# Attention on TensorE: scores and weighted sums over all four channel quarters in turn, in bursts of half a group

## The chip, the core and the metric

The kernel runs on one core of a Trainium2 chip. The metric is device time in microseconds (us): the median of five runs is 6176.71 us (6159.52 to 6181.42). One further execution was recorded by the hardware profiler. Engines are named as in the profile: PE is TensorE (matmuls), PEld its weight loads, DVE is VectorE, ACT is ScalarE, POOL is GpSimd, and SP issues most transfers.

## What is computed

A network of four residual layers on an image tensor of 8 x 56 x 56 x 192 in fp32. Two layers mix tokens by Toeplitz products, the third is a depthwise convolution with an MLP, the fourth is a windowed attention. Only the fourth is touched. Its reference, cut to what matters (x is the group-normalized input):

```python
WS, DISP, N_HEAD, DIM_V, DIM_MODEL = 7, 3, 6, 32, 192
x = jnp.roll(x, (-DISP, -DISP), (1, 2))
b, n_h, n_w, _ = x.shape
wh, ww = n_h // WS, n_w // WS
q, k, v = x @ Wq, x @ Wk, x @ Wv
shp = (b, N_HEAD, wh * ww, WS * WS, DIM_V)          # a plain reshape
q, k, v = q.reshape(shp), k.reshape(shp), v.reshape(shp)
scores = jnp.einsum('bhnqd,bhnkd->bhnqk', q, k) * DIM_V ** 0.5
scores = scores + bias
scores = scores.at[:, :, -ww:].add(LOWER_MASK)
scores = scores.at[:, :, ww - 1:ww].add(RIGHT_MASK)
attn = jax.nn.softmax(scores, axis=-1)
out = jnp.einsum('bhnqk,bhnkd->bhnqd', attn, v)
out = out.reshape(b, n_h, n_w, -1) @ Wfc + bfc
out = jnp.roll(out, (DISP, DISP), (1, 2))
```

So there are 8 x 6 x 64 small attentions of 49 queries by 49 keys, each over 32 channels.

## The kernel before

**Units and groups.** The attention (function `attention`, from L1061) works through 16 units: eight images by two halves of the tokens. A unit is cut into NG = 3 groups of 64 small attentions. The 32 channels of an attention lie on one quarter of the 128 partitions: quarter 0 to 3 hold different attentions, and a group has 16 of them on each quarter.

**One group, by function.**
- `scores` (L1253) is called twice, for i = 0 and i = 1. A call does quarters i and i + 2: for each of 8 windows, two halves (64 rows of the output) and the two quarters it multiplies 32 x 64 weights from `qf` with 32 x 49 columns from `kf` into one PSUM tile `s`. Then comes the softmax's first part: DVE scales and adds the bias (L1274) and takes the maximum (L1283), POOL subtracts it (L1284), ACT takes the exponential (L1285).
- `divide` (L1288): DVE sums (L1292) and takes the reciprocal (L1293), POOL multiplies (L1294).
- `turned` (L1296) transposes the probabilities of the group before on PE (L1300); the copy to SBUF, `et`, is made by DVE for i = 0 (L1310) and by ACT for i = 1 (L1308).
- `weighted` (L1313), also called for i = 0 and i = 1, multiplies 49 x 32 weights from `v` with 49 columns from `et` into the PSUM tile `po`, and `sixths` (L1330) copies `po` out by DVE (L1332) and rearranges it by ACT (L1337).

Scores thus use tiles of the array of 32 rows by 64 columns, and a call touches four of the eight such tiles. Weighted sums use tiles of 64 rows by 32 columns, again four of eight in a call.

**Pieces between.** `project` (L1170) is a generator that makes the next unit's `v`, `qf` and `kf` in ten pieces: four for `v` (L1179, L1189; copied out by ACT, L1197, and sent through DRAM), six for `qf` and `kf` (L1232; copied out by DVE, L1247, and ACT, L1245). `out` (L1341) is the output projection of the unit before, in two pieces (L1348; added to the input by DVE, L1359). The loop (L1402 on) puts such pieces between the bursts, by the table `order` at L1401: in group 0 four pieces of `v`; in group 1 a piece of `qf`, then the first piece of `out` with a piece of `qf`, then the second piece of `out`; in group 2 the last four pieces. The order in a group is

```
scores 0, piece 0, divide 0, scores 1, piece 1, divide 1,
transposes 0 and 1, piece 2, weighted 0, piece 3, weighted 1
```

where transposes and weighted sums belong to the group before (`late`). The loop runs once more after the last unit, for the weighted sums and the output that are left. At the end of group 2 the unit after next is normalized (L1154 on DVE, L1162 on ACT).

**PSUM.** Every PSUM tile comes from `bank2`, four tiles of two banks used in rotation, so a tile can be written once the fourth before it has been read. The instructions of an engine are issued in the order that the framework's scheduling gives; on PE this is the source's order here, on DVE mostly so.

Of the kernel before, what the change touches and what calls it, by code (L numbers as in the profile page):

```python
# [33 lines left out]
def view(ap, offset, dims):  # L34

    return bass.AP(ap.tensor, ap.offset + offset, [ap.ap[0], *dims])


class Net:
# [1021 lines left out]
    def attention(self, L, xs, gn3, gnd, ys, vd):  # L1061
# [6 lines left out]
        nc, tc, inp = self.nc, self.tc, self.inp  # L1068
# [4 lines left out]
        WR = 49  # L1073
        NG = 3
        p = self.at1
        if True:
            one = lambda name, shape: p.tile(shape, F32, name=name, bufs=1)
            bank2 = self.bank2
            gr = [one(f"gr{i}", [128, 4, 2]) for i in range(2)]

            def load_gr(i):
                for half in HALF:
                    nc.sync.dma_start(gr[i][half], gnd[i].rearrange("(b c) s -> c b s", c=C)[128:C])
# [166 lines left out]
                    fs.append(f)  # L1250
                return v, fs[0], fs[1]

            def scores(hh, g, i, qf, kf):  # L1253


                s = bank2()
                for n in range(8):
                    for half in range(2):
                        for c in range(2):
                            qd = slice(32 * (i + 2 * c), 32 * (i + 2 * c) + 32)  # L1260
                            u = (16 * g + 8 * half + n) * WR
                            nc.tensor.matmul(
                                s[64 * half : 64 * half + 64, c, n * WR : (n + 1) * WR],
                                qf[qd, u : u + 64],
                                kf[qd, u : u + WR],
                                start=True,
                                stop=True,
                            )
                var = {0: 1, 3: 2}.get((2 * i + 3 * hh + g) % 4, 0)
                e = ering[count[0] % NE]  # L1270
                count[0] += 1
                ev = e[:, :, :, :WR]
                e3 = e.rearrange("p c n k -> p (c n) k")[:, :, :WR]
                nc.vector.scalar_tensor_tensor(  # L1274
                    ev,
                    view(s, 0, [[512, 2], [WR, 8], [1, WR]]),
                    math.sqrt(32.0),
                    view(bias, var * 8 * WR, [[0, 2], [WR, 8], [1, WR]]),
                    ALU.mult,
                    ALU.add,  # L1280
                )
                mx = p.tile([128, 16], F32, name="mx", bufs=6)
                nc.vector.tensor_reduce(mx, e3, AX.X, ALU.max)  # L1283
                nc.gpsimd.tensor_sub(e3, e3, view(mx, 0, [[1, 16], [0, WR]]))  # L1284
                nc.scalar.activation(e3, e3, AF.Exp)  # L1285
                return e

            def divide(e):  # L1288

                e3 = e.rearrange("p c n k -> p (c n) k")[:, :, :WR]  # L1290
                sm = p.tile([128, 16], F32, name="sm", bufs=6)
                nc.vector.tensor_reduce(sm, e3, AX.X, ALU.add)  # L1292
                nc.vector.reciprocal(sm, sm)  # L1293
                nc.gpsimd.tensor_mul(e3, e3, view(sm, 0, [[1, 16], [0, WR]]))  # L1294

            def turned(e, i):  # L1296
                pt = bank2()
                for c in range(2):
                    for m in range(4):
                        nc.tensor.transpose(  # L1300
                            pt[:113, c, m * 128 : m * 128 + 113],
                            e.rearrange("p c n k -> p c (n k)")[:113, c, m * 128 : m * 128 + 113],
                            self.ident[:113, :113],
                        )
                et = self.at2.tile([113, 8, 113], F32, name="et", bufs=3)
                ev = pt.rearrange("p c (m q) -> p (c m) q", q=128)[:113, :, :113]
                if i:
                    nc.scalar.copy(et, ev)  # L1308
                else:
                    nc.vector.tensor_copy(et, ev)  # L1310
                return et

            def weighted(g, i, et, v, po):  # L1313

                for m in range(4):
                    for half in range(2):
                        for c in range(2):
                            for par in range(2):
                                at = slice(64 * par, 64 * par + WR)
                                qr = i + 2 * c  # L1320
                                u = 4 * half + m
                                nc.tensor.matmul(
                                    po[32 * qr : 32 * qr + 32, par, u * WR : (u + 1) * WR],
                                    v[at, qr, 8 * g + u, :],
                                    et[at, 4 * c + m, 64 * half : 64 * half + WR],
                                    start=True,
                                    stop=True,
                                )

            def sixths(g, po, ot, oj):  # L1330

                nc.vector.tensor_copy(  # L1332
                    view(ot, 16 * WR * g, [[WR, 2], [2 * WR, 8], [1, WR]]),
                    view(po, 0, [[512, 2], [WR, 8], [1, WR]]),
                )
                t0, t1 = 16 * WR * g // 6, 16 * WR * (g + 1) // 6
                nc.scalar.copy(  # L1337
                    view(oj, t0, [[HT, 6], [1, t1 - t0]]), view(ot, 6 * t0, [[1, 6], [6, t1 - t0]])
                )
# [31 lines left out]
            def step(gen):  # L1371

                try:
                    next(gen)
                except StopIteration as end:
                    return end.value
                return None

            units = [(b, hh) for b in (0, 1, 4, 5, 2, 3, 6, 7) for hh in range(2)]
# [10 lines left out]
            for i in range(NE):  # L1390
                e = self.at2.tile([128, 2, 8, 64], F32, name=f"e{i}", bufs=1)
                nc.gpsimd.memset(e, 0.0)
                ering.append(e)
            now = None
            while now is None:
                now = step(gen)
# [5 lines left out]
            for n in range(len(units) + 1):  # L1402
                if n < len(units):
                    (b, hh), (v, qf, kf) = units[n], now
                gen = project(*units[n + 1]) if n + 1 < len(units) else None
                outs = None
                now = None
                for g in range(NG):
                    if g == 1 and n:
                        outs = out(*units[n - 1], *raws.pop(n - 1), oj)  # L1410

                    def give(at):
                        got = now
                        for kind in order[g][at]:
                            if kind and outs is not None:
                                step(outs)
                            elif not kind and gen is not None:
                                got = step(gen)
                        return got

                    es = []
                    for i in range(2):
                        if n < len(units):
                            es.append(scores(hh, g, i, qf, kf))
                        now = give(i)
                        self.norm_part()
                        if n < len(units):
                            divide(es[i])
                    if late is not None:
                        g_late, es_late, v_late = late  # L1430
                        ets = [turned(e, i) for i, e in enumerate(es_late)]
                    now = give(2)
                    if late is not None:
                        if g_late == 0:
                            ot = self.at2.tile([128, HR], F32, name="ot", bufs=1)
                            oj = self.at2.tile([128, 6, HT], F32, name="oj", bufs=1)
                        po = bank2()
                        weighted(g_late, 0, ets[0], v_late, po)
                    now = give(3)
                    if late is not None:  # L1440
                        weighted(g_late, 1, ets[1], v_late, po)
                        sixths(g_late, po, ot, oj)
                    late = (g, es, v) if es else None
                    if g == 0 and n + 3 == len(units) // 2:
                        for more in self.all_norms():
                            pass
                        load_gr(1)
                    if g == 1 and n + 2 < len(units):
                        raws[n + 2] = load(*units[n + 2])
                    if g == 2 and n + 2 < len(units):  # L1450
                        normalize(units[n + 2][0], *raws[n + 2])
# [189 lines left out]
```

## Time and profile before

| what | us |
|---|---|
| median of 5 runs | 6176.71 |
| the profiled execution | 6181.42 |
| its span, first to last instruction | 6179.5 |
| PE busy | 5697.1 (92%) |
| PE weight loads busy | 4462.3 (72%) |
| DVE busy | 2847.8 (46%) |
| ACT busy | 2155.2 (35%) |
| POOL busy | 640.5 (10%) |

The attention's scores begin at 5271.7 us of the span and its units fill the rest. Busy times of its main instructions, from the groups by line from 4900 us on:

| line | what | instructions | busy us, mean ns of one |
|---|---|---|---|
| L1262 PE | scores | 6144 | 118.9, 223 |
| L1322 PE | weighted sums | 6144 | 91.8, 209 |
| L1300 PE | transposes | 768 | 94.4, 274 |
| L1274 DVE | scale, bias | 96 | 91.7, 955 |
| L1283 DVE | maximum | 96 | 92.5, 963 |
| L1292 DVE | sum | 96 | 93.1, 970 |
| L1284 POOL | subtract | 96 | 146.0, 1521 |
| L1294 POOL | multiply | 96 | 146.1, 1522 |
| L1285 ACT | exponential | 96 | 83.9, 874 |

The profile is read like this. Busy time is the union of an engine's instructions; several matmuls can be under way on PE at once, so the mean of one matmul (223 ns) is much longer than the distance between two starts. "<-" names what ended the idle time before an instruction; "issue" is idle time in which the profile shows nothing that was awaited. In instructions in order of time, a row stands for a run of the same kind: start, length, engine, line, operation, output <- inputs, shapes, count. PEclk is the share of the full TensorE clock that was granted; it was 0.96 over the span.

### The profile page before, as it was taken

What the parts mean: (1) busy time and instruction counts of PE and PEld (TensorE: products, weight loads), DVE (VectorE), ACT (ScalarE), POOL (GpSimd) and SP (SyncE); (2) the same over time, 40 slices, a digit from 0 to 9 for tenths busy, and PEclk for the clock granted to TensorE, in tenths of its full rate; (3) what the DMA queues carried; (4) which work ended last, traced back from release to release, by engine and by line L of the source; (5) the groups of instructions that cost most, each with busy time, mean ns of one, the idle gap of its engine ahead of it and who ended that gap; (6) DMA issues with size and microseconds to landing.
All of it is one profiled execution on the core that took longest, in us unless ns stands there. A gap on an engine that the chain in (4) does not pass through costs nothing.

```text
span 6179.5 us, 151657 instructions
## 1 busy us (share of the span) xinstructions
PE 5697.1 (92%) x68704; PEld 4462.3 (72%) x68704; DVE 2847.8 (46%) x4862; ACT 2155.2 (35%) x2738; POOL 640.5 (10%) x833
## 2 busy tenths in 40 slices
PE   5998999899999999999899889999999999988997
PEld 3777778788788788788778778985665444666665
DVE  6554555444556444555444443242222321555565
ACT  2334434223444323344323332224323433333332
POOL 0000000000000000000000110000000100333332
PEclk9899999999999999999999999999999999999998
DMA  7799987888685788786898856653453322434442
GB/s 261 164 220 255 267 228 223 230 233 237 190 212 178 204 238 238 184 218 183 226 243 260 244 178 220 222 201 127 154 175 127 92 63 61 74 85 96 87 91 60
DMA packets 1139556, 1119.74 MB, mean 181 GB/s; under 512 B 342528, under 2 KB 1076736, under 8 KB 1123488
## 3 DMA queue, kind: packets, MB, share of 16 engines
q1 hardware_dynamic: 1103328, 909.05, 54.6%
q0 software_dynamic: 35584, 200.98, 10.3%
q8 instruction: 540, 8.85, 0.6%
q14 instruction: 104, 0.85, 0.0%
HBM read 753.79 MB, written 389.15 MB: 185 GB/s over the span
## 4 chain that ended last, share of the span: by engine, by line
PE 72%; DVE 11%; DMA 7%; ACT 4%; issue 3%; SPq 2%; POOL 2%; DVEq 0%; POOLq 0%; ACTq 0%; another core or an unknown queue 0%
PE bank L257 14%; PE bank L394 7%; PE bank L958 6%; PE bank L511 6%; PE bank L521 5%; PE bank L411 5%; PE bank L819 5%; PE bank L1038 4%; DMA qv<-t 3%; PE bank L526 3%; PE bank L543 3%; PE bank L1052 3%; DVE t L266 2%; PE bank L1179 2%; POOL e L1284 1%
## 5 line engine op out<-in xcount | busy, mean ns | idle before, releaser
L257 PE MATMUL bank<-wq,t 128*128 128x256 f32 (+4 forms) x7680 | 1275.0, 373 | 34.3 <-DVE t L266 14.4
L257 PEld LDWEIGHTS bank<-wq,t 128*128 128x128 f32 (+2 forms) x7680 | 1002.8, 190 | 277.0 <-issue 111.0
L295 ACT ACTIVATE t<-t 128x2048 f32<-128x2048 f32 (+2 forms) x288 | 427.7, 1489 | 749.4 <-DVE t L266 743.9
L401 ACT COPY ot<-bank 128x896 f32<-128x896 f32 x576 | 483.8, 921 | 398.1 <-PE bank L394 387.9
L266 DVE TENSOR_TENSOR t<-bank,wq 128x1024 f32<-128x1024 f32 (+3 forms) x480 | 518.3, 1112 | 202.0 <-PE bank L257 199.8
L394 PE MATMUL bank<-q,tm 56*64 56x112 f32 x18432 | 519.9, 265 | 73.7 <-issue 46.8
L555 ACT ACTIVATE t<-bank,wo 128x448 f32<-128x448 f32 x448 | 247.9, 635 | 895.0 <-PE bank L526 870.9
L394 PEld LDWEIGHTS bank<-q,tm 56*64 56x64 f32 x18432 | 480.1, 137 | 108.3 <-issue 77.7
L411 PE MATMUL bank<-ident,ot 120*128 120x120 f32 x4032 | 479.7, 278 | 70.8 <-ACT ot L401 38.6
L298 DVE TENSOR_TENSOR t<-t 128x1024 f32<-128x1024 f32 (+2 forms) x288 | 274.5, 956 | 577.9 <-ACT t L295 458.4
L411 PEld LDWEIGHTS bank<-ident,ot 120*128 120x128 f32 x4032 | 438.5, 147 | 119.8 <-ACT ot L401 44.2
L511 PE MATMUL bank<-t,wo 128*128 128x224 f32 x1792 | 391.6, 373 | 45.5 <-DVE t L493 43.3
L958 PE MATMUL bank<-z,w 128*128 128x448 f32 (+1 forms) x1344 | 414.1, 555 | 4.3 <-ACT h L967 4.3
L565 DVE SCALAR_TENSOR_TENSOR t<-bank,wo,t 128x448 f32<-128x448 f32 x112 | 76.4, 682 | 702.0 <-PE bank L550 701.2
L511 PEld LDWEIGHTS bank<-t,wo 128*128 128x128 f32 x1792 | 348.8, 201 | 63.9 <-issue 40.5
L521 PE MATMUL bank<-t,wo 128*128 128x224 f32 x1792 | 363.6, 356 | 13.3 <-issue 6.8
L582 DVE TENSOR_TENSOR t<-t,t 128x896 f32<-128x896 f32 x224 | 235.7, 1083 | 300.5 <-ACT t L555 300.5
L521 PEld LDWEIGHTS bank<-t,wo 128*128 128x128 f32 x1792 | 340.6, 192 | 21.3 <-issue 12.9
L819 PEld LDWEIGHTS bank<-xt,cm 113*112 113x112 f32 x3072 | 312.1, 179 | 36.6 <-issue 30.5
L958 PEld LDWEIGHTS bank<-z,w 128*128 128x128 f32 (+1 forms) x1344 | 182.6, 189 | 208.4 <-issue 197.6
L819 PE MATMUL bank<-xt,cm 113*112 113x108 f32 (+2 forms) x3072 | 320.4, 265 | 4.0 <-ACT h L967 2.9
L427 POOL DMA_DIRECT2D L_sum<-s x288 | 141.7, 498 | 1739.1 <-DVE s L417 1736.6
(147 smaller groups left out, 7088.0 us busy)
## 6 DMA issues: line engine op xcount, KB each, us to landing
q<-qv SPq DMA_DIRECT2D x36, 3584.0 KB
q<-qv SPq DMA_DIRECT2D x72, 1568.0 KB
L_sum<-s POOLq DMA_DIRECT2D x288, 392.0 KB, 7.8
t<-L_sum SPq DMA_DIRECT2D x112, 1008.0 KB
qv<-t SPq DMA_DIRECT2D x192, 512.0 KB
cm<-in_L_cm SPq DMA_DIRECT2D x96, 896.0 KB
tm<-L_mat SPq DMA_DIRECT2D x72, 896.0 KB
x<-t POOLq DMA_DIRECT2D x112, 336.0 KB, 5.4
```

The costliest lines, as they stand in the source:

```text
L257: nc.tensor.matmul(pp[:m, b, 256 * j : 256 * j + k], x[rows, j, 2 if part else b, s : s + m], w[rows, part, c0 + c : c0 + c + k],  start=p ...
L266: nc.vector.tensor_add(z[:m, c : c + k, :], view(pp[:m], 0, [[1, k], [256, 4]]), view(bias[:m], c0 + c, [[1, k], [0, 4]]),)
L295: nc.scalar.activation(z[:m, :n, :], z[:m, :n, :], AF.Silu)
L298: nc.vector.tensor_mul(prod[:m, :k], half[:, :, 0], half[:, :, 1])
L394: nc.tensor.matmul(pt[64 * s : 64 * s + 64, r, j * 112 : (j + 1) * 112], tm[rows, c * H : c * H + 64], q[rows, PR * s : PR * s + PR, 4 * c ...
L401: nc.scalar.copy(view(ot, 4 * g, [[112 * 32, 2], [32, 112], [1, 4]]), view(pt, 0, [[512, 2], [1, 112], [112, 4]]),)
L411: nc.tensor.transpose(pz[:, i, :120], ot[:120, at : at + 128], self.ident[:120, :120])
L511: mm(gs[c // 2][:, b, c % 2 * 256 : c % 2 * 256 + N], pw[:, 0, 128 * c : 128 * c + 128], xn[:, b], start=c % 2 == 0, stop=False,)
L521: mm(P[:, b, :N], ow[:, c, 0:128], g[:, 4 * b + c], start=c == 0, stop=False)
L555: nc.scalar.activation(pg[:, c], view(gs[i], c * 256, [[512, 2], [1, N]]), AF.Silu, bias=pb[:, 2 * i + c : 2 * i + c + 1],)
L819: nc.tensor.matmul(pc[:, 128 * e + 4 * m0 : 128 * e + 4 * m1], cm[:113, e, k, :], xt[:, m0 - 1 + k : m1 - 1 + k, c + e, :], start=n == 0 a ...
L958: nc.tensor.matmul(phs[c][:, s, :TT], w0[rows, part, at : at + 128], z[rows, Z[2 if part else s], :], start=part == flip, stop=part != flip,)
```

## The change

Three things move; no matmul is added or dropped, and each has the operands it had.

1. `scores` fills both PSUM tiles of a group (quarters 0 and 2 in the one, 1 and 3 in the other) in two parts. A part does four of the eight windows for all four quarters, the quarter changing fastest. The softmax, now a function of its own, follows for both tiles after the second part.
2. `weighted` is cut the same way: a part does two of the four window pairs for all four quarters, so its first part needs both `et` tiles.
3. In the loop the pieces and the two `divide` calls change places with these parts. The order in a group becomes

```
scores part 0, piece 0, scores part 1, softmax 0 and 1, piece 1,
divide 0 and 1, transposes 0 and 1, piece 2, weighted part 0,
piece 3, weighted part 1
```

The core of the diff:

```diff
-            def scores(hh, g, i, qf, kf):
-                s = bank2()
-                for n in range(8):
+            def scores(hh, g, qf, kf, part, ss):
+                for n in range(4 * part, 4 * part + 4):
                     for half in range(2):
-                        for c in range(2):
+                        for i, c in ((0, 0), (1, 0), (0, 1), (1, 1)):
                             qd = slice(32 * (i + 2 * c), 32 * (i + 2 * c) + 32)
                             u = (16 * g + 8 * half + n) * WR
                             nc.tensor.matmul(
-                                s[64 * half : 64 * half + 64, c, n * WR : (n + 1) * WR],
+                                ss[i][64 * half : 64 * half + 64, c, n * WR : (n + 1) * WR],
                                 qf[qd, u : u + 64],
                                 kf[qd, u : u + WR],
                                 start=True,
                                 stop=True,
                             )
+
+            def softmax(hh, g, i, s):
...
-            def weighted(g, i, et, v, po):
-                for m in range(4):
+            def weighted(g, ets, v, po, part):
+                for m in range(2 * part, 2 * part + 2):
                     for half in range(2):
                         for c in range(2):
-                            for par in range(2):
+                            for i in range(2):
+                                for par in range(2):
...
                     es = []
-                    for i in range(2):
-                        if n < len(units):
-                            es.append(scores(hh, g, i, qf, kf))
-                        now = give(i)
-                        self.norm_part()
-                        if n < len(units):
-                            divide(es[i])
+                    if n < len(units):
+                        ss = [bank2(), bank2()]
+                        scores(hh, g, qf, kf, 0, ss)
+                    now = give(0)
+                    self.norm_part()
+                    if n < len(units):
+                        scores(hh, g, qf, kf, 1, ss)
+                        es = [softmax(hh, g, i, s) for i, s in enumerate(ss)]
+                    now = give(1)
+                    self.norm_part()
+                    for e in es:
+                        divide(e)
...
                         po = bank2()
-                        weighted(g_late, 0, ets[0], v_late, po)
+                        weighted(g_late, ets, v_late, po, 0)
                     now = give(3)
                     if late is not None:
-                        weighted(g_late, 1, ets[1], v_late, po)
+                        weighted(g_late, ets, v_late, po, 1)
                         sixths(g_late, po, ot, oj)
```

## The prediction

> **What bounds the kernel now.** I read the page first, then the busy time by stretch, then who TensorE waits for, then TensorE's instructions in order of time. From the page:
>
> ```profile
> span 6179.5 us, 151657 instructions
> ...
> PE 5697.1 (92%) x68704; PEld 4462.3 (72%) x68704; DVE 2847.8 (46%) x4862; ACT 2155.2 (35%) x2738; POOL 640.5 (10%) x833
> ...
> q8 instruction: 540, 8.85, 0.6%
> ```
>
> TensorE (PE) is busy 92% of the span, no other engine half of it. The last line counts to the argument below: 540 packets, 8.85 MB, so 16 KB of instructions a packet; 68704 matmuls with 68704 weight loads, over 540, are 254 a packet. The change touches the attention alone, and its steady part is this stretch:
>
> ```profile
> 5290.00:6106.00 816.00, 732.25 (x20356) 553.21 (x20352) 483.81 (x777) 282.50 (x347) 267.24 (x189) 0.96 0.41 87
> ```
>
> The columns are length, then busy time of PE, PEld, DVE, ACT and POOL, the granted clock, and DMA. PE is busy 732 of 816 us. The remainder, by who ended it (us in total, times, longest):
>
> ```profile
> PE bank L1262 <- issue: 20.1, 20, 3.1
> PE bank L1300 <- DVE ra L1359: 18.7, 13, 1.9
> PE bank L1322 <- DVE et L1310: 15.2, 14, 2.0
> PE bank L1232 <- issue: 11.5, 15, 1.3
> ```
>
> So two chains over VectorE cost 34 us, and "issue", where nothing was awaited, costs about as much. What those issue gaps are is seen in order of time (start, length, instructions, idle before):
>
> ```profile
> 5415.00 1.57 PE L1322 MATMUL bank<-et,v 49*32 49x49 f32 x128
> 5416.50 0.72 PE L1262 MATMUL bank<-f,f 32*64 32x49 f32 x33
> 5418.80 0.68 PE L1262 MATMUL bank<-f,f 32*64 32x49 f32 x31 [1.58 <-issue]
> 5419.41 1.55 PE L1232 MATMUL bank<-xa,Wq 128*32 128x224 f32 x32
> 5420.88 0.96 PE L1232 MATMUL bank<-xb,Wq 64*32 64x224 f32 x32
> 5421.77 0.68 PE L1262 MATMUL bank<-f,f 32*64 32x49 f32 x32
> 5423.02 0.68 PE L1262 MATMUL bank<-f,f 32*64 32x49 f32 x32 [0.56 <-issue]
> ```
>
> From gap to gap stand 31+32+32+32 = 127 matmuls, with as many weight loads 254 instructions: one packet. I followed this through the stretch: the 38 issue gaps over 0.25 us all stand at multiples of that count, together 37 us, each 2.3 to 5.9 us (median 4.2) after the block before it began. I read them as TensorE waiting for its next block of instructions: a block used up in under some 4 us is followed by a gap.
>
> **Part 1, the bursts.** Each matmul of the source makes two records, so a quarter's scores, and each half group after the change, are 64 records. A scores burst today:
>
> ```profile
> 5436.36 1.15 PE L1262 MATMUL bank<-f,f 32*64 32x49 f32 x64 [0.30 <-DVE f L1247]
> 5437.44 1.55 PE L1179 MATMUL bank<-Wv,xa 128*112 128x192 f32 x8
> ```
>
> It takes 1.08 us until the next work starts; from first to last start 1.15 - 0.22 (one matmul, median) = 0.93. A weighted burst, by the same view, is 0.90 - 0.20 = 0.70. Now four tiles of the array are cycled through (two row quarters by two halves of the columns; two row halves by two column quarters); after the change eight. Number and size of the matmuls stay. The trace has no scores on eight tiles; the nearest row has the same 32*64 tiles, all eight, in the output projection:
>
> ```profile
> 5354.77 2.50 PE L1348 MATMUL bank<-oj,wfc 32*64 32x224 f32 x88 [0.33 <-ACT f L1245]
> ```
>
> (2.50 - 0.35)/87 = 24.7 ns each for 224 columns, 0.110 ns a column; its sister on four 32*128 tiles took (3.57 - 0.49)/37 = 83 ns for 392, 0.212. Eight tiles run at 1.9 times the rate. Bounds: no gain at all, and twice as fast. I take 0.46 us off a scores burst and, as starts never lie closer than 6.7 ns (64 x 6.7 = 0.43), 0.27 off a weighted one. Four bursts a group: 1.46 us, x 48 groups = 70 us; 63 of it in the stretch above.
>
> A rule speaks against this: the Trainium skill, TensorEngine Tiling (Array Packing), Instruction Overhead, gives every matmul some 60 cycles whatever its free size, and advises against tiling a dimension that is already small. At 2.4 GHz this is an estimated 25 ns each, 1.6 us a burst, and the change would gain nothing: 6177 us. The row shows 0.93 us for 64, so I don't follow it.
>
> **Part 2, what eats it: blocks of instructions.** The instruction count and its order by bursts stay, so blocks keep their contents. In the stretch 38 blocks end in a gap: what is saved in them only lengthens the gap. They hold 19 us of the 63. 51 more took 4.2 us or less and would be gapped when shortened: 25 us, of which I keep half. The 70 longer ones hold 19 us, kept. Sum 31 us, half of the saving; bounds 0 and 63.
>
> **Part 3, PSUM.** Four tiles of two banks rotate; a new one waits for the reader of the fourth before it. With both score tiles taken first, the order is s0, s1, p0, p1, t0, t1, p2, po, p3. Then p0, the first piece, waits for `po` of the group before, freed by VectorE's copy L1332 (0.97 us) after the last weighted burst: W ends 5451.13, copy 5451.20 to 5452.17; the piece could start at about 5452.25 and today starts at 5452.14. So the first score burst's 0.46 us is lost in two groups of three: 32 x 0.46 = 15 us. Behind the last weighted burst of the third group the scores wait for `f` (the 0.30 above), whose copy stands behind the normalization on VectorE: its 0.27 x 15 = 4 us is hidden. These 19 us sit where bursts sit, and half of those were lost already: 9.5 us off. t1 waits for s1's reader, 3.1 us after the scores; TensorE gets there after 3.2: nothing, and 0.5 us in 15 groups, 8 us, where a copy of `f` (L1247, 0.61) delays VectorE. In group 1 `out` takes its second tile from s0's reader, so TensorE stops 1.0 us after the scores. Its cover is the wait of L1300 for L1359 (18.7 us, 13 times): VectorE works from the scores' end to L1359's start in 8.2 us now, in 2 x 1.94 (L1274, L1283) + 1.52 (POOL) + 0.88 (ACT) + 0.97 + 0.25 and hand-overs = 7.95 then. Nothing; without the cover 15 us.
>
> **Part 4, softmax later.** Both quarter pairs' L1274, L1283, L1284, L1285 now follow the second burst; behind them on VectorE queue the sums and L1310, for which the weighted matmuls wait, now for both quarters' copies at once. From the end of the second burst: 4.15 us for four VectorE steps, POOL to 5.77, exp to 6.68, ACT's copy (L1308, 0.90) to 7.6. In a Wq/Wk group TensorE arrives after 2.37 + 1.77 + 2.37 = 6.5, a wait of 1.2; today 15.2 us in 15 such groups, 1.0. I take no change; bounds -15 us (all of it goes) and the third rival's price. In a Wv group VectorE puts L1310 ahead of the second sum today (5445.03 against 5448.34) and TensorE doesn't wait; I expect the same. In the last unit, with no pieces, the second maximum (6147.64) stood behind the first sum (6146.76), which waited for exp; it now comes first, and the second L1300 (6156.45) can follow the first (6151.81, 1.62 long): 3 us gained. No DMA is added or moved past another, and norm_part is called as often as before.
>
> **Sum.** Profiled execution 6181.4 us (span 6179.5 + 1.9). 6181.4 - 31 + 9.5 - 3 = 6156.9. That run lies 4.7 over the median of 6176.7, so 6152.
>
> **Rivals.** *Nothing comes through (6165 to 6185):* either eight tiles run no faster, so the change doesn't do what it says (+3 us for p0), or the block supply takes the 25 us of the short blocks too (12 less: 6165). For it: the 51 blocks just above the limit. Against: 70 long ones. *All comes through (6177 - 70 = 6107):* the issue gaps would have to shrink with the bursts. Against: their even spacing. *Slower:* VectorE issues L1310 behind the second quarter's sum in Wv groups too. Then the copy ends at 6.72 + 0.97 + 1.09 = 8.8 us after the scores and TensorE, there after 2.32 + 1.77 + 2.32 = 6.4, waits 2.5 us: x 16 = 40; in Wq/Wk groups 2.4 against 1.0: 21. 61 - 24.5 = +36: 6213. It decides from the point where both kinds of group do so; Wq/Wk groups alone (which have that order today, 5429.92 before 5430.80) leave 6173. Against it: in Wv groups the transposes are done at 3.3 us, long before that sum can start.
>
> The granted clock could shift any of these: 0.50 in 5411.5 to 5414.8, where another unit's 88 matmuls of that row took 4.18 instead of 2.50 us. One more such stretch a unit is 15 x 1.7 = 25 us. The Trainium skill, TensorE: Matmul & The Clock Gate (Why this matters for your kernels), says that idle gaps of over some 3 us between bursts halve the clock; here gaps of 1 to 3 us preceded some of the halved stretches, and the rule would add none of my terms.
>
> **How the numbers follow.** Forecast (6130 to 6167) 0.55, nothing through 0.16, all through 0.07, slower 0.22. A run of this kernel can tell about 0.3%, 18.5 us, from no change: of the forecast some 0.43 lies beyond it. Faster 0.50, same 0.28, slower 0.22. The range runs from all through to the slower case: 6107 to 6213.
>
> **What would show it.** L1262 and L1322 bursts of 64 in about 0.68 and 0.63 us instead of 1.15 and 0.90 (part 1); issue gaps over 37 us (part 2); the first piece waiting for L1332 (part 3); `out` waiting for L1274 while L1300's wait for L1359 shrinks; L1322's wait for L1310 or L1308 near 1 us in Wq/Wk groups, none in Wv groups (part 4). Bursts of old length, issue gaps near 80 us, or waits of 2.5 us at L1322 in every group would prove me wrong.

## The result, and the profile after

The changed kernel takes 6179.68 us (median of 29 runs, 6165.14 to 6199.54) against 6176.29 us of the kernel before on the same chips (51 runs, 6159.52 to 6190.12). The ratio is 1.0004 with a 95% interval of 0.9997 to 1.001: no change that can be measured. The forecast of 6152 us did not come true. The time lies in the stretch of the rival "nothing comes through", though not for the reasons given there alone.

The lines of the page and of the steady stretch that answer to those of before, first the page:

```profile
span 6175.9 us, 151672 instructions
...
PE 5665.4 (92%) x68704; PEld 4427.9 (72%) x68704; DVE 2848.6 (46%) x4862; ACT 2156.3 (35%) x2737; POOL 638.1 (10%) x833
```

Matmuls are as many as before, and PE is busy for 32 us less. The profiled execution took 6177.83 us. Now the steady stretch (length, busy time of PE, PEld, DVE, ACT and POOL, clock, DMA), and under it who TensorE waits for there:

```profile
5290.00:6106.00 816.00, 706.48 (x20328) 528.32 (x20320) 484.20 (x776) 284.90 (x347) 265.15 (x190) 0.95 0.42 86
```

```profile
PE bank L1261 <- issue: 30.0, 20, 2.5
PE bank L1302 <- DVE ra L1362: 22.4, 14, 2.2
PE bank L1232 <- issue: 16.6, 16, 1.8
PE bank L1261 <- DVE f L1247: 13.2, 13, 1.3
PE bank L1325 <- ACT et L1310: 10.9, 13, 1.3
PE bank L1325 <- issue: 7.4, 11, 1.5
```

L1261, L1302, L1325, L1351, L1310 and L1362 are L1262, L1300, L1322, L1348, L1308 and L1359 of before. PE is busy for 25.8 us less than before in the stretch, and does the same amount of work in it (20328 against 20356 matmuls). So all that was saved is idle time now. "Issue" has gone from 38 to 55 us; the 47 issue gaps over 0.25 us lie, as before, multiples of some 127 matmuls apart, the content of one packet of instructions. A wait of the scores for `f`, 2 us before, is 13. The wait of the transposes for L1362 is 4 us longer, and that of the weighted sums for `et` 4 us shorter.

What a burst does is seen in windows of 0.25 us of the scores alone (length, busy PE with its matmuls, PEld, clock, DMA). A matmul lasts 0.22 us, so those under way at a boundary are counted twice. First the changed kernel, then the kernel before:

```profile
5429.50:5429.75 0.25, 0.25 (x30) 0.25 (x33) 1.00 0.00 0
5429.75:5430.00 0.25, 0.25 (x46) 0.25 (x33) 1.00 0.00 0
```

```profile
5436.36:5436.61 0.25, 0.25 (x16) 0.25 (x19) 1.00 0.00 0
5436.61:5436.86 0.25, 0.25 (x32) 0.25 (x27) 1.00 0.00 0
```

Before, 16 matmuls start in each window. After, 30 start in the first and only some 17 in the second (46 less some 29 still running): twice the old pace for about 32 matmuls, then nearly the old one. Over all scores bursts of 64 at full clock in the stretch, the first 32 starts span 0.26 us and the last 32 starts 0.39 us in the median; before, 0.46 and 0.43. From first to last start a scores burst of 64 takes 0.67 us (before 0.93), a weighted burst 0.67 (before 0.70).

The new wait for `f` is best seen at the step from the `qf`/`kf` pieces to the next unit (start, length, engine, line, output <- inputs, count, idle before):

```profile
5424.87 3.02 POOL L1296 TENSOR_TENSOR e<-e,sm 128x784 f32<-128x784 f32 x2 [2.21 <-DVE sm L1295]
...
5426.72 2.18 DVE L1154 TENSOR_SCALAR xa<-ra,gn 128x1484 f32<-128x1484 f32 x2 [1.39 <-PE bank L1232]
...
5428.83 0.61 DVE L1247 COPY f<-bank 128x448 f32<-128x448 f32 x1
...
5429.50 0.89 PE L1261 MATMUL bank<-f,f 32*64 32x49 f32 x64 [1.27 <-DVE f L1247]
```

The last copy of `f` (L1247) stands behind the normalization (L1154) on VectorE. The normalization starts while GpSimd multiplies (until 5427.89) and takes 2.18 us instead of 1.29, so TensorE waits 1.27 us for the scores' operands where it waited 0.30 before. In 13 of the last 14 units the longer L1154 takes 1.62 to 1.95 us after the change; in the 14th it takes 1.06, as in all units before. The longest, the last of the three durations in ns in the summary of this line, is 1057 before and 1955 after:

```profile
L1154 DVE TENSOR_SCALAR xa<-ra,gn x32: 317/688/1057, 4796.8 to 6054.5; 128x1484 f32<-128x1484 f32 x16, 128x84 f32<-128x84 f32 x16
```

```profile
L1154 DVE TENSOR_SCALAR xa<-ra,gn x32: 309/686/1955, 4791.6 to 6052.0; 128x1484 f32<-128x1484 f32 x16, 128x84 f32<-128x84 f32 x16
```

### The profile page after: what moved, and what is told of

It is laid out like the page before. It is cut to its first block, busy times and chain, and to the rows that moved or that the text cites. A ratio compares the mean times of both kernels' runs of the same rounds, so it can differ in the third digit from the quotient of the medians.

```text
span 6175.9 us, 151672 instructions
## 1 busy us (share of the span) xinstructions
PE 5665.4 (92%) x68704; PEld 4427.9 (72%) x68704; DVE 2848.6 (46%) x4862; ACT 2156.3 (35%) x2737; POOL 638.1 (10%) x833
## 4 chain that ended last, share of the span: by engine, by line
PE 73%; DVE 9%; DMA 7%; issue 4%; ACT 4%; SPq 1%; POOL 1%; DVEq 0%; another core or an unknown queue 0%; POOLq 0%; ACTq 0%
PE bank L257 14%; PE bank L394 7%; PE bank L958 6%; PE bank L511 6%; PE bank L521 5%; PE bank L411 5%; PE bank L819 5%; PE bank L1038 4%; DMA qv<-t 3%; PE bank L526 3%; PE bank L543 3%; PE bank L1052 3%; PE bank L1232 2%; DVE t L266 2%; PE bank L1261 1%
## 5 line engine op out<-in xcount | busy, mean ns | idle before, releaser
L257 PE MATMUL bank<-wq,t 128*128 128x256 f32 (+4 forms) x7680 | 1282.1, 374 | 40.4 <-DVE t L266 16.7
L521 PEld LDWEIGHTS bank<-t,wo 128*128 128x128 f32 x1792 | 340.2, 192 | 21.7 <-issue 13.7
```

The lines of the kernel that those rows point to most:

```text
L257: nc.tensor.matmul(pp[:m, b, 256 * j : 256 * j + k], x[rows, j, 2 if part else b, s : s + m], w[rows, part, c0 + c : c0 + c + k],  start=p ...
L521: mm(P[:, b, :N], ow[:, c, 0:128], g[:, 4 * b + c], start=c == 0, stop=False)
```

## The experiments

Twelve kernels were run. Two theories were set against each other first. SUPPLY: the bursts really are shorter, and instruction blocks that come too late, with the new wait for `f`, take that back. ORDER: the late softmax and the PSUM order cost what the bursts gain. This table has eleven of them (supply_probe measures something else and stands below); "attention" is the time from the first scores to the end of the profiled execution (one each), the middle columns are its parts in us (wait for `ra` and `rb`, for `et`, for VectorE's writes of `f` and `xa`, for GpSimd's products `e`), and "half" is time at half the TensorE clock, added up from windows of 1 us.

| kernel | attention | PE busy | issue | ra | et | f, xa | e | half | ratio to before (95%) |
|---|---|---|---|---|---|---|---|---|---|
| before | 907.8 | 801.7 | 43.0 | 23.7 | 18.1 | 3.5 | 5.6 | 112 | 1 |
| after | 909.4 | 773.1 | 63.5 | 29.3 | 16.6 | 14.4 | 0.2 | 120 | 1.0004 (0.9997 to 1.001) |
| order_only | 905.8 | 802.2 | 37.3 | 26.8 | 17.2 | 3.5 | 3.4 | 113 | 0.9989 (0.9979 to 0.9999) |
| sums_only | 942.3 | 811.2 | 56.4 | 13.7 | 40.0 | 3.2 | 5.5 | 154 | 1.0057 (1.0044 to 1.007) |
| mixed_after | 912.3 | 767.0 | 83.6 | 33.0 | 6.8 | 10.8 | 0.2 | 127 | 1.0024 (1.0013 to 1.0035) |
| norm_behind | 911.8 | 779.3 | 61.4 | 23.7 | 16.1 | 19.4 | 0.4 | 137 | 1.0021 (1.0007 to 1.0034) |
| norm_first | 900.6 | 773.2 | 64.8 | 27.9 | 16.5 | 4.4 | 0.4 | 120 | 0.9994 (0.9983 to 1.0005) |
| scores_only | 899.8 | 771.4 | 59.8 | 29.7 | 2.7 | 22.9 | 1.1 | 99 | 1.0005 (0.9992 to 1.0017) |
| scores_norm | 881.5 | 768.4 | 58.8 | 26.1 | 3.6 | 8.6 | 1.3 | 88 | 0.9973 (0.9964 to 0.9982) |
| spread_before | 895.2 | 790.9 | 38.5 | 34.1 | 0 | 1.2 | 21.9 | 83 | 0.9983 (0.9975 to 0.9992) |
| spread_even | 852.3 | 777.0 | 29.1 | 3.3 | 0.2 | 1.7 | 22.1 | 55 | 0.9909 (0.989 to 0.9928) |
| mixed_spread | 850.0 | 777.5 | 28.0 | 5.9 | 0 | 2.2 | 16.7 | 62 | 0.9914 (0.9899 to 0.9929) |
| mixed_spread8 | 907.3 | 772.8 | 20.1 | 9.0 | 0 | 1.1 | 86.1 | 110 | 1.0015 (1.0005 to 1.0025) |

Where attention and ratio differ by more than a few us (scores_only), the ratio, with its many runs, has the last word on the time; the trace tells which waits moved.

### order_only: the new order with the old bursts

```diff
-                for n in range(4 * part, 4 * part + 4):
+                for n in range(8):
-                        for i, c in ((0, 0), (1, 0), (0, 1), (1, 1)):
+                        for i, c in ((part, 0), (part, 1)):
```

and in `weighted` all four `m` with `i` = `part`.

> The changed kernel's order (late softmax, both score tiles taken first, pieces between), but a burst again covers one pair of quarters, so four tiles of the array, as before the change. Theory SUPPLY (the bursts' gain is real but smaller than forecast, and comes back as issue gaps between blocks of 256 instructions, and as one new wait for f): bursts of old length (scores 1.15, weighted 0.90 us), TensorE's busy time in the steady stretch back up by 26 us to about 732, issue gaps back from 55 to about 38 us, the wait for f still near 13; the attention 915 to 920 us long, some 8 over both kernels. Rival ORDER (the late softmax and the PSUM order cost the whole gain of 25 us, whatever the bursts): waits for ra, et and f together 25 us above those of before, attention about 933 us.

Attention 905.8 us, ratio 0.9989: the order of parts, pieces and PSUM tiles costs nothing, and that half of ORDER falls. The busy time came back as SUPPLY said (733 us in the stretch), and the issue gaps went down to 32:

```profile
PE bank L1325 <- DVE et L1312: 15.9, 12, 2.6
PE bank L1261 <- issue: 15.5, 16, 2.4
PE bank L1232 <- issue: 9.2, 9, 2.8
PE bank L1325 <- issue: 6.9, 7, 1.5
...
PE bank L1261 <- DVE f L1247: 1.7, 6, 0.3
```

SUPPLY was wrong about `f`: its wait is gone too, and L1154 takes 1.05 us in all units. VectorE's queue shows why this run is milder than its name: the first tile is complete after the first burst, so the scheduler puts its softmax there, and VectorE's order is that of the kernel before. The late softmax comes with the eight-tile scores only, so this run doesn't test it; scores_norm and mixed_spread8 below do, together with those bursts.

### sums_only: eight tiles for the weighted sums alone

The kernel before, with `weighted` and its two calls taken from the changed kernel.

> The kernel before, with only the weighted sums in bursts over all four quarters (eight tiles); scores and softmax stay as before. SUPPLY: the weighted burst of 64 records hardly shortens (0.90 to about 0.85 us), 96 bursts give under 5 us, the attention 903 to 908 us. The forecast's own size (0.27 us a burst) would give 26 us: attention about 882, or about 895 with half of it lost in issue gaps. ORDER: 908, since the order of the softmax isn't touched.

35 us slower by the ratio, against all three expectations. The bursts of 64 do shorten, from 0.70 to 0.60 us from first to last start. Each half now needs both copies `et`, and the one that ScalarE makes comes last. TensorE begins a burst with four matmuls and then stops:

```profile
5458.73 0.28 PE L1323 MATMUL bank<-et,v 49*32 49x49 f32 x4
5460.77 0.77 PE L1323 MATMUL bank<-et,v 49*32 49x49 f32 x60 [1.77 <-ACT et L1308]
```

```profile
PE bank L1262 <- issue: 29.7, 23, 3.5
PE bank L1323 <- ACT et L1308: 23.6, 13, 2.2
PE bank L1323 <- DVE et L1310: 12.2, 10, 1.8
```

Before, the first burst needed the copy for i = 0 alone. In the attention the waits for `et` are 22 us longer, the issue gaps 13, and 42 more us pass at half clock, with PE busy for 10 us more.

### mixed_after: thin and dense pieces in turn

In `project`, the pieces as two functions, called in the order of a string:

```diff
+                kinds = "qvqqvvqvqq" if (b, hh) != (0, 0) else "vvvvqqqqqq"
+                for at, kind in enumerate(kinds):
+                    piece, args = todo[kind].pop(0)
+                    piece(*args)
```

> The changed kernel with the ten pieces of a projection in mixed order (q v q q, v v, q v q q, where q is a piece of qf or kf with 128 PE instructions and v a piece of v with 32 in the same 2.5 us), so that dense and thin blocks of instructions alternate. SUPPLY: issue gaps in the steady stretch fall from 55 to 20 to 40 us and the attention shortens by about as much, 875 to 895 us. ORDER: issue gaps may move, but the waits for VectorE's chain stay or grow, since every group now has q pieces whose f copies stand in VectorE's queue: attention 905 to 920.

The issue gaps rose instead, by 20 us; the ratio is 1.0024. How dense the stream is over a whole group does not set the gaps. The bursts that still stand next to each other, the last weighted one and the first scores one, are 256 instructions in some 1.6 us. They stand so in the changed kernel too, so why the gaps grew here stays open:

```profile
PE bank L1334 <- issue: 32.2, 27, 3.4
...
PE bank L1270 <- issue: 25.7, 22, 2.9
PE bank L1235 <- issue: 20.1, 13, 3.3
```

(L1334, L1270 and L1235 are the weighted sums, the scores and the `qf`/`kf` pieces here.)

### norm_behind and norm_first: the stall behind GpSimd

In norm_behind the normalization is put behind the last copy of `f` in VectorE's queue; in norm_first the same call stands ahead of the last `weighted`, and so ahead of the copy `ot` as well.

```diff
-                        normalize(units[n + 2][0], *raws[n + 2])
+                        with self.tc.issue_after(last_f[0].ins):
+                            normalize(units[n + 2][0], *raws[n + 2])
```

> The changed kernel with the two normalizing instructions of VectorE (L1154) put behind the last copy of f in VectorE's queue. In the changed kernel the longer one of the two takes 1.95 us instead of 1.05 in 12 of 14 units, each time with a multiplication on GpSimd (L1296) under way as it starts, and the copy of f, for which the scores wait, stands behind it. If that is the source of the new wait: it falls from 13.2 to about 2 us, the normalization takes 1.05 us again or costs nothing, and the attention shortens by 8 to 12 us, to 898 to 901. If the copy of f is late for another reason (its matmuls end late), nothing changes: 909.

The wait for `f` went, and a wait for `xa` took its place:

```profile
PE bank L1181 <- DVE xa L1154: 16.1, 14, 1.5
```

The scheduler had put the copy `ot` between the two normalizing instructions, so the next unit's first piece (L1181) was late: ratio 1.0021. L1154 took 1.05 us in all units, so the diagnosis stood and the cure did not. Hence norm_first:

> The changed kernel with both normalizing instructions of VectorE directly behind the last copy of f, and ahead of the copy of the weighted sums (in norm_behind the latter had slipped between the two, and the next piece waited 16 us for the second). If the stall of VectorE behind GpSimd's multiplication is what made f late: the longer instruction takes 1.05 us, the waits for f and for xa together fall from 13 (norm_behind: 17) to under 6 us, attention 899 to 903 against 909.4. If something else is behind it: 907 to 912.

As expected: attention 900.6 us, 8.8 us less than the changed kernel, and the longest L1154 is 1055 ns. The ratio of 0.9994 is 1.0 thousandth lower than the change's, with intervals that overlap: the stall and its cure are shown by L1154 and by the wait, a gain in the whole time is not.

### scores_only and scores_norm: eight tiles for the scores alone

The changed kernel with `weighted` by pairs, as in order_only; scores_norm has norm_first's edit as well.

> The changed kernel with the eight-tile bursts for the scores alone; the weighted sums go by pairs of quarters again, as in order_only. So it differs from order_only in the scores' bursts alone. Theory SUPPLY (bursts really shorten, instruction blocks then arrive too late, and that gives most of it back): scores bursts 0.67 instead of 0.93 us from first to last start, busy time in the steady stretch 25 us under order_only's 733, issue gaps 15 to 20 us over its 32, attention 896 to 904 against its 905.8. Rival TILES (eight tiles cost time by something else than late instructions, as the 35 us that sums_only lost may say): issue gaps as in order_only, or attention 908 and more. If the gain were whole: 881.

> scores_only with norm_first's order on VectorE: eight-tile bursts for the scores alone, and both normalizing instructions directly behind the last copy of f. It takes the stall behind GpSimd out of scores_only, where the waits for f were 23 us, and shows what is left of the bursts' 25 us against order_only's attention of 905.8 us. If the stall simply adds up: the wait for f under 4 us, attention 879 to 884. If supply and the next wait take it (issue gaps stay near 60, and the wait for et, 17 us in order_only and 3 in scores_only, comes back): 892 to 899. In both cases L1154 takes 1.05 us again.

Without the stall cured, attention is 899.8 us, as SUPPLY expected, but the ratio is 1.0005. Issue gaps are 21 us above order_only's, and L1154 is worse than in the changed kernel: even its short form of 84 columns, 0.31 us elsewhere, takes 1.51 us in 9 of 15 units, about as long as one product on GpSimd (1.52).

```profile
PE bank L1261 <- DVE f L1247: 21.0, 14, 2.3
```

```profile
L1154 DVE TENSOR_SCALAR xa<-ra,gn x32: 310/1510/2370, 4800.5 to 6055.3; 128x1484 f32<-128x1484 f32 x16, 128x84 f32<-128x84 f32 x16
```

With the stall taken off the path (scores_norm) attention is 881.5 us, within the expectation for "simply adds up", and the ratio 0.9973: 17 us faster than the kernel before. L1154 itself is still 1.7 us long in several units, other than expected, but now nothing but the next piece stands behind it (6.8 us). The issue gaps stayed at 59. The wait for `et` did not come back, since VectorE now has the copy `et` ahead of both sums in the groups where it mattered, as in the changed kernel. In norm_first, which differs only in its weighted sums, it is there (norm_first, then scores_norm):

```profile
PE bank L1327 <- ACT et L1312: 11.0, 14, 1.3
```

```profile
PE bank L1327 <- ACT et L1312: 0.6, 2, 0.4
```

So not all of scores_norm's gain comes from faster bursts. Against order_only PE is busy for 34 us less, but issue gaps are 21 us longer; the wait for `et` is 14 us shorter, and 25 us less pass at half clock, which probably makes up part of the smaller busy time. In the stretch, scores_only has 24 us less busy time than order_only and 21 us more of issue gaps: what faster bursts alone leave is a few us, within the uncertainty.

### supply_probe: the pace of instructions, measured by itself

```diff
+            for r in range(16):
+                scores(1, 0, qf, kf, r % 2, ss)
+            for r in range(16):
+                four(0, qf, kf, r % 2, ss[r % 2])
```

`four` is the old burst of 64 over four tiles; nobody reads these 2048 extra matmuls.

> The changed kernel with extra work behind the last unit that nobody reads: 16 bursts of scores over eight tiles (1024 matmuls, 1024 weight loads) and then 16 bursts over four tiles (as many), with nothing between them. It measures the rate at which TensorE gets instructions. SUPPLY: both parts take the same time, about 3.3 to 3.6 us per 256 instructions, 27 us a part, each block a burst and then a gap of issue. If TensorE itself were the limit: 1024 x 10.7 ns = 11 us for eight tiles and 1024 x 14.8 ns = 15 us for four, without gaps.

The extra bursts over eight tiles are L1261, those over four L1276:

```profile
6176.53 2.15 PE L1261 MATMUL bank<-f,f 32*64 32x49 f32 x128 [2.51 <-issue]
6180.27 2.16 PE L1261 MATMUL bank<-f,f 32*64 32x49 f32 x128 [1.59 <-issue]
6184.02 2.15 PE L1261 MATMUL bank<-f,f 32*64 32x49 f32 x128 [1.59 <-issue]
...
6198.72 2.94 PE L1276 MATMUL bank<-f,f 32*64 32x49 f32 x128 [0.80 <-issue]
6202.47 2.94 PE L1276 MATMUL bank<-f,f 32*64 32x49 f32 x128 [0.81 <-issue]
6205.94 2.94 PE L1276 MATMUL bank<-f,f 32*64 32x49 f32 x128 [0.53 <-issue]
```

128 matmuls and 128 weight loads, a block, start every 3.75 us (6184.02 - 6180.27), over eight tiles as over four (6202.47 - 6198.72); the closest two are 3.47 us apart (6205.94 - 6202.47). What differs is the gap, mostly 1.59 against 0.80 us. Here faster bursts buy nothing at all: blocks come no faster. The clock was 0.50 through both parts, so the pace of blocks at full clock is not measured here; and about a quarter of the eight-tile matmuls had run earlier, in among the last unit's work. (In the attention of the kernels above the 16 KB packets of instructions follow each other at 3.24 us at the closest, and where a gap comes before a block, its first matmul mostly starts 1.2 to 1.8 us after the last packet ended, 1.4 to 1.5 in the median.)

### spread_before and spread_even: keeping the bursts apart

The kernel before, with `turned` moved to the head of the group, so that pieces or transposes stand between all bursts; spread_even changes the middle group's slots as well:

```diff
-            order = (((0,), (0,), (0,), (0,)), ((0,), (1, 0), (1,), ()), ((0,), (0,), (0,), (0,)))
+            order = (((0,), (0,), (0,), (0,)), ((1,), (0,), (1,), (0,)), ((0,), (0,), (0,), (0,)))
```

> The kernel before with the transposes of the group before moved to the head of the group, so that a group is: transposes, scores 0, piece, scores 1, piece, weighted 0, piece, weighted 1, piece. Now the last weighted burst and the first scores burst (256 instructions in 1.6 us) have the piece and the transposes between them. SUPPLY: issue gaps in the steady stretch fall from 38 to under 20 us; the wait for et (15 us) goes, since 6 us of work lie between transposes and weighted sums; attention 870 to 890 against 907.8. Rival CHAIN: the transposes now wait for the probabilities, since only 9 us lie between the second scores burst and them and the softmax takes 7.6 in a free queue: a wait of 1 to 3 us for GpSimd's L1294 in most of 48 groups, attention 908 to 960.

Half right: 11 us faster by the ratio, the wait for `et` gone, and a wait for GpSimd's `e` of 16 us more in its place. Issue gaps in the stretch fell to 34 only: a `qf` piece (128 instructions) with a burst (128) is a block of 3.4 us, still a little under the probe's 3.47 to 3.75 (at half clock).

```profile
PE bank L1348 <- DVE ra L1359: 33.1, 27, 2.4
PE bank L1262 <- issue: 14.7, 15, 2.2
PE bank L1300 <- POOL e L1294: 13.4, 15, 2.8
PE bank L1232 <- issue: 11.6, 18, 2.6
```

> spread_before with the middle group's slots changed: the two pieces of the output projection stand in slots 0 and 2 instead of 1 and 2, with a piece of q and k in slots 1 and 3. In spread_before the second of them waits 33 us for L1359 (the tiles of the first, four before it), and a slot in that group is empty. Expected by PSUM rotation: this wait falls from 37 to under 8 us, issue gaps stay near 34, attention 865 to 877 against 895. If VectorE's queue rather than the rotation sets that wait: it moves to another line, attention 890 to 900.

More than expected: attention 852.3 us, ratio 0.9909 (56 us), the fastest by a tie with mixed_spread, and faster than both kernels.

```profile
PE bank L1300 <- POOL e L1294: 22.1, 18, 4.6
PE bank L1322 <- issue: 14.9, 15, 1.9
PE bank L1232 <- issue: 9.0, 14, 1.4
PE bank L1232 <- ACT f L1245: 8.1, 17, 0.6
PE bank L1348 <- DVE ra L1359: 3.3, 10, 0.5
```

The wait for L1359 is gone, as the expectation had it. Against spread_before that wait is 31 us shorter, the issue gaps 9 us, and PE is busy for 14 us less with the same bursts. The expectation left out the last two. The smaller busy time goes with the clock, 55 us at half clock instead of 83 (112 in the kernel before); that the clock is its cause is argued.

### mixed_spread and mixed_spread8

spread_even with mixed_after's order of pieces, and then with the eight-tile scores put back.

> spread_even with the pieces of a projection in mixed order (q v q q, v v, q v q q) instead of four v and then six q. SUPPLY in its sharper form, from the probe (a block of 256 instructions every 3.74 us at most, one block ahead): a group of four q pieces has 1056 instructions, 4.1 blocks, 15.4 us, for 14.8 us of work; a mixed group has 960, 14.0 us. Issue gaps in the steady stretch fall from some 34 to under 18 us, attention 10 to 25 us shorter than spread_even's. Rival, since mixed_after raised the gaps from 55 to 77: alignment decides, and gaps stay at 30 or more.

No difference to spread_even: attention 850.0 us, and issue gaps of 27.5 us in the stretch, where spread_even has 27.8; under 18 were expected, and 30 or more by the rival. With mixed_after this takes down the theory's sharper form, that the density of a whole group sets the gaps.

> mixed_spread with the eight-tile bursts of the scores and the late softmax (the change's first half) put back. In this rotation a piece behind the second scores burst of the middle group waits 1.1 us for the first scores tile's reader, 16 us in all. SUPPLY: where blocks come in time, the bursts' 25 us of busy time are a real gain and issue gaps grow by under 10 us; so attention is 0 to 15 us shorter than mixed_spread's, the 16 us paid. Rival CHAIN: the late softmax makes the transposes wait for GpSimd's products in most groups (some 1 us each, 40 us): attention 15 to 40 us longer than mixed_spread's, whatever the bursts save. If issue gaps grow by 20 us and more in spite of the thinner stream: supply still takes it all.

CHAIN, and more than it expected, 57 us longer instead of 15 to 40: the transposes wait 86 us for GpSimd's products, because the eight-tile scores make the whole softmax start after the second burst. All of spread_even's gain is lost (ratio 1.0015), though the issue gaps are the shortest of all, 20 us. Whether the bursts would pay in this order with an earlier softmax stays open: a softmax by half tiles, which could start after the first burst, wasn't tried.

```profile
PE bank L1311 <- POOL e L1305: 65.6, 81, 2.2
PE bank L1334 <- issue: 13.8, 20, 1.4
```

## Why the prediction was right and wrong

The runs can be put in a row; the second step changes three things at once:

| from, to | what differs | attention, us | by the ratios, us |
|---|---|---|---|
| before, order_only | order of parts and pieces | -2.0 | -7 |
| order_only, scores_norm | scores on eight tiles, softmax after both bursts, normalization behind `f` | -24.3 | -10 |
| scores_norm, norm_first | weighted sums on eight tiles | +19.1 | +13 |
| norm_first, after | normalization ahead of `f`, stalled behind GpSimd | +8.8 | +6 |
| sum | | +1.6 | +2 |

(The last column is the difference of ratios times 6176 us; each has an uncertainty of some 6 to 10 us.) So in the profiled executions the change is one gain and two losses. By the ratios the weighted sums' loss is the clearest; the 6 us of the normalization lie within the uncertainty, and the gain of 10 us barely beyond it. Step by step:

**Part 1 (bursts): the mechanism right, the size wrong.** The term "0.46 us off a scores burst, 0.27 off a weighted one, 63 us in the stretch" was mis-sized: it measured 0.26 and 0.03 us, and PE is busy for 26 us less in the stretch. Why the weighted sums gain so little stays open; in sums_only they gained 0.10. The 24.7 ns a matmul of the output projection, from which the factor 1.9 came, has 224 columns behind each instruction. With 49 columns the first 32 starts span 0.26 us, some 8 ns each, and the last 32 starts 0.39 us, some 13. What slows the rest is not shown. It doesn't depend on a wait for instructions just before: in the changed kernel 61 matmuls behind an issue gap of 1.93 us took 0.64 us, the first 32 of them again 0.26. The rule of the Trainium skill that the prediction set aside (TensorEngine Tiling (Array Packing), Instruction Overhead: some 60 cycles a matmul, an estimated 25 ns) does not fit: 0.67 us for 64 is 10.5 ns each. Its conclusion, no gain, came true in the sum, for other reasons.

**Part 2 (blocks): right in kind, the share too small.** Issue gaps did take much of what was saved, in the stretch 16.5 us over before and 22 over order_only, of 26. The share was taken as half and was 0.63 to 0.85. supply_probe shows such a limit by itself, at half clock. Parts 1 and 2 together left 4 to 9 us of busy time not taken back, where the sum had 31: this is most of why the forecast was missed.

**Part 3 (PSUM): wrong, and harmless.** It took for granted that a tile waits for the reader of the fourth one before. The first piece was to wait for the copy of `po` (15 us in all); in the trace it starts before that copy ends, without a gap ahead of it, so it does not wait for it. That the piece has another tile is the likely reason, but the trace doesn't name buffers:

```profile
5443.66 0.97 DVE L1335 COPY ot<-bank 128x784 f32<-128x784 f32 x1 [1.87 <-PE bank L1325]
```

```profile
5444.41 1.55 PE L1232 MATMUL bank<-xa,Wq 128*32 128x224 f32 x32
```

Nor does `out` wait for L1276. What Part 3 called hidden behind `f` (4 us) became the new wait: the prediction saw that the copy of `f` stands behind the normalization (L1154), but took the normalization's length from the trace of before, where GpSimd was idle beside it. That is the missed step, 9 us in the profiled executions (after against norm_first), 6 us by the ratios.

**Part 4 (softmax later): mostly right.** The weighted sums wait 0.8 us in Wq/Wk groups (10.9 in 13) where 1.2 were expected, and not in Wv groups; the last unit gained some 5 us (wait for `e` 5.6 to 0.2) where 3 were expected. It missed that the weighted sums on eight tiles keep a wait that the later softmax would have removed. With the sums by pairs the wait for `et` is 3.6 us (scores_norm), with all quarters at once 16.5 (norm_first), since ScalarE's copy, behind both exponentials, is needed for the first half.

**The wait for `ra`.** It was expected to hold or shrink and grew from 18.7 to 22.4 us. L1362 stands at the end of VectorE's chain, 8.2 us after the scores' end, as in the kernel before; shorter work in between only lets TensorE arrive earlier (argued).

**Rivals.** "Nothing comes through" gave two reasons, bursts that run no faster and blocks that take the short ones too. The first did not hold for the scores and nearly held for the weighted sums, the second held in good part, and the wait for `f` made up much of the rest. "Slower" did not come: VectorE puts `et` ahead of the sums in the Wv groups and in the last (Wq/Wk) group of a unit; in the middle group `et` comes behind them, without a wait for it. The clock moved by 8 us of half-clock time, worth an estimated 4 us.

## What to carry to other kernels

Making a burst of small matmuls faster pays only if the instructions for what follows are there: count how many instructions lie between two stretches of long matmuls, and spread short bursts among long work before shortening them. Joining two bursts that fed two separate chains joins the chains too: the first consumer then waits for the later producer (here both `et` copies, and both halves of the softmax). When a reorder puts a VectorE instruction beside GpSimd work that it never met before, its old duration is no longer a safe number.

## What the runs showed of the hardware that was not expected

- TensorE gets its instructions in blocks of 256 (16 KB). With nothing else to wait for and the clock at 0.50, one came every 3.47 to 3.75 us in steady running, whether a block's work took 2.15 or 2.94 us. In the attention, packets follow each other at 3.24 us at the closest.
- L1154 (fp32, SBUF to SBUF) takes 1.05 us alone. With a product on GpSimd under way as it starts it takes up to 1.95 in the changed kernel, and ends 0.79 us after that product (5428.68 against 5427.89), in all 14 such units. The Trainium skill, SBUF — State Buffer (SBUF: two separate sides), says that VectorE and GpSimd share a port pair under an exclusive lock, held for a whole instruction; the trace agrees as far as VectorE's end follows the product's.
- In the probe the clock was 0.50 for 50 us, though in its second part TensorE was busy for 80% (23.93 of 30 us) and no gap was longer than 0.98 us. The Trainium skill, TensorE: Matmul & The Clock Gate (Why this matters for your kernels), names idle gaps of over some 3 us as what to avoid; here the clock stayed halved without any such gap in that part, and what keeps it there is not shown. In the attention, half-clock time went with the waits: 154 us in sums_only, 55 in spread_even.
